# Second attention: key sums in two PSUM banks by turns, preparation and mixing on two shared ones, rows of q loaded place by place

## The chip, the cores and the metric

The program runs on one core of one Trainium2 chip. The metric is the device time of one execution in microseconds; lower is better. TensorE is called PE below, VectorE DVE, ScalarE ACT, GpSimd POOL; SP is the sync engine, whose queue issues most of the DMAs.

## The reference, cut to what matters

The program computes two layers over `x` of 4 batches x 512 tokens x 128: each layer is a layer norm, an attention `s`, a feed-forward net of 8 experts with two chosen, and `x = x + s * silu(ffn)`. The change touches the second layer's attention alone: 16 heads of width 8, and for each of 16 "wavelengths" a softmax of the same scores under another scale.

```python
def _L1_attn_ref(x, Wq, bq, Wk, bk, Wv, bv, Wo, bo, phase_modulators, interference_weights):
    Q, K, V = proj(Wq, bq), proj(Wk, bk), proj(Wv, bv)     # B, 16 heads, S, 8
    cos_pm = jnp.cos(phase_modulators)
    def wl_step(acc, wl):
        cpm, iw = wl
        m = cpm[None, :, None, None]
        scores = jnp.einsum('bhqd,bhkd->bhqk', Q * m, K * m) * SCALE
        scores = scores * jnp.cos(KERR * scores * scores)
        attn = jax.nn.softmax(scores, axis=-1)
        return (acc + jnp.einsum('bhqk,bhkd->bhqd', attn, V) * iw, None)
    ...
    return jnp.einsum('bse,ef->bsf', combined, Wo) + bo
```

## The kernel before

**What stands for the 16 softmaxes.** For small scores the exponential under every scale is a sum of six functions of the same score: three exponentials (of one, two and three times a fixed step) and the square, the score itself and one. So the kernel computes three arrays from each block of scores: `e0` by an exponential on ACT, `e1` as its square on ACT, `e2` as their product on DVE (line 1572), and sums each over the keys against V with a column of ones. The other three functions need no array per pair of query and key: the square of a score is a quadratic form in q, the score a linear one. `feat` holds the products of k's elements that this takes (5 shifts of 8 products, 8 linear ones and a one, in `ROWS1` = 49 columns), `forms` (line 1281) sums them over the keys against V into `lin`, `features1` (line 1326) makes the same products of q in `rows1`, and `bank1` (line 1348) multiplies the two. `sums1`, `quotients1` and `output1` then mix numerators and denominators over the wavelengths and apply `Wo`.

**Rounds.** `attn1` (line 1583) runs 64 rounds, 16 for a batch: round i stands for 4 heads (a group m of four) and 128 keys; 4 rounds make a group, 4 groups a batch. t is the round's place in its batch. In round i the program issues, each engine's part in this order: the scores of round i+1 (PE), the copy `bank0` of the last group's sums (DVE, where t is a multiple of 4), the evictions on ACT of what the last round's chunk left, the 24 instructions of `over_keys` (PE, the group `acc`), the chunk of this place, `e0` of i+1 (ACT), the rests on DVE and POOL of the last round's chunk, `e1` (ACT) and `e2` (DVE) of i+1. Where t is a multiple of 4, the chunk's PE part stands between the scores and `over_keys`.

**Chunks.** `prepare1` gives pieces for the next batch by place: token projections 0, 1 and 13, projections by head 2 and 3, `forms` 5, 7, 10 and 11. `mixing` gives `sums1` at 1 and 10, `quotients1` at 5, 6, 13 and 14, `bank1` at 8 and 15, `output1` at 9, partly for the batch before. Batch 0 has no mixing of a batch before, batch 3 no preparation.

**PSUM.** Of the eight banks, scores have four (tag `s`), the sums over keys one (`acc`), mixing two (`mix`), preparation one (`prep`). All engines keep the order in which the program records their instructions.

**Loads.** `project("q")` writes the transposed q to DRAM (`qe`, each head group twice in a row, so that shifted windows are contiguous). For each half batch `features1` loads `rows` (6 copies of 8 rows for each of two halves, 48 partitions) and `other` (5 shifted windows, 40 partitions), with 4 DMAs on SP, and the two operands are multiplied on POOL (line 1345). `operands1` loads q and k of a group (`q<-qd`, `k<-kd`), two groups ahead. `other` is one buffer for all halves. SP's queue takes its DMAs in order and holds all of them: parts of k and q (`kd`, `qd`), `qe`, `rows`, `other`, q, k and the output.

Of the kernel before, what the change touches and what calls it, by code (L numbers as in the profile page):

```python
# [12 lines left out]
F32 = mybir.dt.float32  # L13
# [52 lines left out]
LINEAR = SHIFTS * D1  # L66
ROWS1 = LINEAR + D1 + 1
# [30 lines left out]
class Kernel:  # L98
# [927 lines left out]
    def heads1(self, pool, keep):  # L1026


        nc = self.nc
        of = {}  # L1030
        for each in (32, WL):
            m = pool.tile([P, 4], F32, name=f"of{each}")
            nc.gpsimd.memset(m, 1.0)
            for at in range(0, P, each * 4):
                part = m[at : at + each * 4]
                nc.gpsimd.affine_select(
                    out=part, in_=part, pattern=[[-each, 4]], compare_op=ALU.is_ge, fill=0.0,
                    base=0, channel_multiplier=1,
                )
                nc.gpsimd.affine_select(  # L1040
                    out=part, in_=part, pattern=[[each, 4]], compare_op=ALU.is_ge, fill=0.0,
                    base=each - 1, channel_multiplier=-1,
                )
            of[each] = m


        self.count = keep.tile([P, 3], F32, name="count")
        ranges = (
            (0, SCALE1**2 * 2.0, ((D1, 4 * D1, SCALE1**2), (0, LINEAR, 0.0))),
            (1, SCALE1, ((LINEAR, LINEAR + D1, 0.0),)), (2, 1.0, ((LINEAR + D1, ROWS1, 0.0),)),  # L1050
        )
        for slot, value, limits in ranges:
            nc.gpsimd.memset(self.count[:, slot : slot + 1], value)
            for at in (0, HALF):
                part = self.count[at : at + HALF, slot : slot + 1]
                for first, end, fill in limits:
                    nc.gpsimd.affine_select(
                        out=part, in_=part, pattern=[[0, 1]], compare_op=ALU.is_ge, fill=fill,
                        base=-first, channel_multiplier=1,
                    )  # L1060
                    nc.gpsimd.affine_select(
                        out=part, in_=part, pattern=[[0, 1]], compare_op=ALU.is_ge, fill=fill,
                        base=end - 1, channel_multiplier=-1,
                    )
        return of
# [93 lines left out]
    def begin1(self):  # L1159

        nc, keep = self.nc, self.keep1
        self.bounds = keep.tile([P, 2 * B * H1 + 2], F32, name="bounds")

        self.feat = keep.tile([P, 4, H1, ROWS1], F32, name="feat")
        nc.gpsimd.memset(self.feat[:, :, :, ROWS1 - 1 : ROWS1], 1.0)
        self.sets1 = []
        for k in range(2):
            strip = keep.tile([P, 4, H1, STRIP], F32, name=f"strip{k}")
            nc.gpsimd.memset(strip, 0.0)
            nc.gpsimd.memset(strip[:, :, :, 26:27], 1.0)  # L1170

            lin = keep.tile([P, 2, 4, 32], F32, name=f"lin{k}")
            nc.gpsimd.memset(lin, 0.0)
            self.sets1.append((strip, lin))


        self.rows1 = [keep.tile([P, 4, S], F32, name=f"rows{mm}") for mm in range(2)]
        self.other1 = keep.tile([P, 4, S], F32, name="other")
        nc.gpsimd.memset(self.other1, 1.0)
        self.now1, self.banks1, self.inv1, self.prod1 = {}, {}, {}, {}  # L1180

    def prepare1(self, b, xnT, psum, tag):
# [9 lines left out]
        def tokens(w):  # L1192
# [9 lines left out]
            def rest(ps):  # L1202
# [13 lines left out]
                if w == "q":  # L1216
                    sq = pool.tile([P, 4 * H1, D1], F32, name=f"tsq{w}{b}", tag="tsq")
                    self.pool1(nc.gpsimd.tensor_mul(sq, t, t))
                    now["squares" + w] = sq
                    return  # L1220
                feat = self.feat.rearrange("p k h r -> p (k h) r")
                self.pool1(nc.gpsimd.tensor_copy(twice[:, :, D1 : 2 * D1], t))
                for d in range(SHIFTS):
                    self.pool1(nc.gpsimd.tensor_mul(
                        feat[:, :, d * D1 : (d + 1) * D1], t, twice[:, :, d : d + D1]
                    ))
                self.pool1(nc.gpsimd.tensor_copy(feat[:, :, LINEAR : LINEAR + D1], t))
                now["squares" + w] = feat[:, :, 0:D1]
# [13 lines left out]
        def project(w):  # L1242
# [10 lines left out]
            def rest(t):  # L1253
                if w == "q":

                    twice = now["twice"] = self.a1d.tile(
                        [4, 2 * D1, 4, S], F32, name=f"qe{b}", tag="qe"
                    )
                    for m in range(4):
                        for k in range(2):  # L1260
                            self.dma1(
                                twice[m, k * D1 : (k + 1) * D1].rearrange("d r s -> r d s"),
                                t[m * 32 : m * 32 + 32],
                            )
# [16 lines left out]
        def forms(mm, first):  # L1281
# [3 lines left out]
            def pe():  # L1285
                ps = psum.tile([P, 2, 9], F32, name=f"pl{b}_{mm}_{first}", tag=tag[0], bufs=tag[1])
                for r in heads:
                    for k in range(4):
                        for o in range(2):
                            h = (2 * mm + o) * 4 + r  # L1290
                            self.mm1(
                                ps[o * HALF : o * HALF + ROWS1, r - first],
                                lhsT=self.feat[:, k, h], rhs=strip[:, k, h, 18:27],
                                start=(k == 0), stop=(k == 3),
                            )
                return ps

            def rest(ps):
                for o in range(2):
                    rows = slice(o * HALF, o * HALF + ROWS1)  # L1300
                    self.vec1(nc.vector.tensor_tensor(
                        lin[rows, mm, first : first + 2, 0:27].rearrange(
                            "p r (x d) -> p r x d", x=3
                        ),
                        bc(ps[rows], 2, 3), bc(bc(self.count[rows], 1, 2), 3, 9), ALU.mult,
                    ))
# [4 lines left out]
            0: tokens("k"), 1: tokens("v"), 2: project("k"), 3: project("q"), 5: forms(0, 0),  # L1311
            7: forms(0, 2), 8: sizes("k"), 10: forms(1, 0), 11: forms(1, 2), 13: tokens("q"),
# [13 lines left out]
    def features1(self, b, mm):  # L1326

        nc, rows, other = self.nc, self.rows1[mm], self.other1
        for o in range(2):
            src, at = self.now1[b]["twice"][2 * mm + o], o * HALF  # L1330
            each = src[0:D1].rearrange("d r s -> d (r s)")
            self.dma1(
                rows[at : at + LINEAR + D1].rearrange("p r s -> p (r s)"), bc(each, 0, SHIFTS + 1)
            )

            (step, _), (one, n) = each.ap
            windows = bass.AP(
                tensor=each.tensor, offset=each.offset,
                ap=[[step, SHIFTS], [step, D1], [one, n]],
            )  # L1340
            self.dma1(other[at : at + LINEAR].rearrange("p r s -> p (r s)"), windows)

# [5 lines left out]
    def bank1(self, b, mm):  # L1348
# [17 lines left out]
        def evict(out):  # L1366
            for o, ps in enumerate(out):
                t = self.a1.tile([P, S], F32, name=f"bank1_{b}_{mm}_{o}", tag="bank1", bufs=3)
# [109 lines left out]
    def end1(self, b, g1):  # L1478
# [7 lines left out]
        den = psum.tile([P, 4, P], F32, name="dene", tag="prep")  # L1486
# [96 lines left out]
    def attn1(self, xnT, g1):  # L1583
# [4 lines left out]
        with tc.tile_pool(name="a1", bufs=2) as self.a1, tc.tile_pool(  # L1588
# [9 lines left out]
            def over_keys(i, f, ex):  # L1598
                b, m, k = i // 16, i // 4 % 4, i % 4
                if k == 0 and f == 0:  # L1600
                    self.acc = psum.tile([P, S], F32, name=f"acc{b}_{m}", tag="acc")
# [9 lines left out]
            def bank0(i):  # L1611

                t = pool.tile([P, S], F32, name=f"bank0_{i}", tag="bank0", bufs=3)
                self.vec1(nc.vector.tensor_copy(t, self.acc))  # L1614
# [22 lines left out]
            loads, makes = {1: [(0, 0)], 4: [(0, 1)]}, {2: [(0, 0, 0), (0, 0, 1)]}  # L1637
            for fb in range(B):
                if fb:
                    loads[fb * 16 - 7], loads[fb * 16 + 1] = [(fb, 0)], [(fb, 1)]  # L1640
                    makes[fb * 16 - 4], makes[fb * 16 - 3] = [(fb, 0, 0)], [(fb, 0, 1)]
                makes[fb * 16 + 6], makes[fb * 16 + 7] = [(fb, 1, 0)], [(fb, 1, 1)]
            waiting, late, prep, products = [], [], {}, {}
            large = self.large1(flag)
            for i in range(n):
# [8 lines left out]
                if t == 0:  # L1654
                    prep = self.prepare1(b + 1, xnT, psum, ("prep", 1)) if b + 1 < B else {}
                for fb, mm, half in makes.get(i, []):
                    products[fb, mm][half]()
                for fb, mm in loads.get(i, []):
                    if fb == 0:
                        for at in (ROWS1 - 1, HALF + ROWS1 - 1):  # L1660
                            self.dma1(self.rows1[mm][at : at + 1], self.other1[at : at + 1])
# [4 lines left out]
                if t % 4 == 0 and i:  # L1666
                    bank0(i)
                ready = evicted(waiting)
                chunks = [c for c in (mixing(b, t), prep.get(t)) if c]
                if t % 4 == 0:  # L1670
                    waiting = [(pe(), *more) for pe, *more in chunks]
                for f, e in enumerate((first, second, third)):
                    over_keys(i, f, e)
                if t % 4:
                    waiting = [(pe(), *more) for pe, *more in chunks]
# [6 lines left out]
                late = [f for f in [rest(x) for rest, x in ready] if f]  # L1682
                if nxt:
# [3 lines left out]
            bank0(n)  # L1687
# [429 lines left out]
```

## Time and profile before

| | us |
|---|---|
| median of 3 runs | 908.65 (904.13 to 909.3) |
| profiled execution, its span | 914.08, 912.0 |
| second attention, rounds 0 to 63 | about 533 to 890 of the span |
| PE busy (whole span) | 832.6, 91% |
| DVE, ACT, POOL busy | 597.1, 519.4, 387.5 |
| mean granted clock of PE | 0.963 |

Times are read against the span's start. A busy PE is not a PE at its peak, since matmuls are pipelined and their ends modelled; the two numbers that matter are when a round's first instruction starts and what an engine waited for before it. A group of instructions is named by what it writes and reads, as in `acc<-e,strip`: the sums over keys. Lines of 321, 324 and 333 are those of helpers that record every matmul, activation and DMA, so groups are told apart by their tiles. Durations by kind in this stage:

| instruction | line | mean us |
|---|---|---|
| `e0` and `e1`, ACT, 128x1024 | 324 | 1.02, 1.06 |
| `e2`, DVE, 128x1024 | 1572 | 1.485 (1.16 to 2.30) |
| `bank<-acc` copy, DVE | 1614 | 0.68 |
| reciprocal `inv`, DVE, 128x256 | 1393 | 1.75 |
| `rows<-rows,other`, POOL, 128x512 | 1345 | 1.70 (1.26 to 2.27) |
| `feat<-tokk`, POOL, 128x512 | 1224 | 1.61 (1.04 to 2.17 over the whole span) |
| issue of `rows<-qe`, `other<-qe`, `qe<-qT`, SP | 333 | 0.72, 0.73, 0.58 (medians) |

### The profile page before, as it was taken

How to read it: one execution, taken by the hardware profiler on the slowest of the kernel's cores; microseconds unless marked ns; L12 is line 12 of the kernel's file. 1: busy time of each engine (PE TensorE's matmuls, PEld its weight loads, DVE VectorE, ACT ScalarE, POOL GpSimd, SP SyncE). 2: the span in 40 equal slices, each digit the busy share in tenths (PEclk: the TensorE clock that was granted, in tenths of full speed). 3: DMA queues.
4: the chain of work that ended last, by engine and by line, in shares of the span. 5: the costliest groups of instructions: out<-in, count | busy, mean ns of one | idle time of the engine just before them, and what ended most of it. 6: DMA issues, size and time to landing. Idle time of an engine off the chain costs nothing. (4 is left out here: it accounts for less than half of the span.)

```text
span 912.0 us, 19106 instructions
## 1 busy us (share of the span) xinstructions
PE 832.6 (91%) x7724; PEld 511.1 (56%) x7724; DVE 597.1 (65%) x1170; ACT 519.4 (57%) x692; POOL 387.5 (42%) x469
## 2 busy tenths in 40 slices
PE   8998899999999999989999998559888989888886
PEld 4666788898897969866777742112232323222324
DVE  7764666666668868835534277538876877677574
ACT  3434465655656665534422388547766777677760
POOL 7840244545444434643060036327825492413212
PEclk9999899999999999999999999879998999899998
DMA  8502221212212121000031021362431243121000
GB/s 215 130 14 67 85 64 44 71 36 71 63 44 72 24 70 32 19 1 1 1 102 62 1 60 50 105 180 70 140 97 50 61 150 89 49 73 38 1 12 16
DMA packets 72719, 57.68 MB, mean 63 GB/s; under 512 B 40000, under 2 KB 64928, under 8 KB 71216
## 3 DMA queue, kind: packets, MB, share of 16 engines
q1 hardware_dynamic: 70432, 54.97, 21.2%
q0 software_dynamic: 1616, 1.16, 0.8%
q8 instruction: 63, 1.03, 0.5%
q10 hardware_dynamic: 576, 0.26, 0.1%
q14 instruction: 32, 0.26, 0.1%
HBM read 36.41 MB, written 19.92 MB: 62 GB/s over the span
## 5 line engine op out<-in xcount | busy, mean ns | idle before, releaser
L1572 DVE TENSOR_TENSOR e<-e,e 128x1024 f32<-128x1024 f32 x126 | 182.0, 1485 | 100.9 <-ACT e L324 98.9
L321 PE MATMUL acc<-e,strip 128*32 128x512 f32 x1520 | 197.8, 643 | 36.1 <-DVE bank L1614 35.6
L324 ACT ACTIVATE e<-s 128x1024 f32<-128x1024 f32 x126 | 122.2, 1024 | 99.0 <-PE s L321 99.0
L321 PEld LDWEIGHTS acc<-e,strip 128*32 128x32 f32 x1520 | 46.6, 115 | 156.3 <-issue 97.2
L324 ACT ACTIVATE e<-e 128x1024 f32<-128x1024 f32 x126 | 126.4, 1061 | 0.0
L324 ACT ACTIVATE h<-ph 128x1024 f32<-128x1024 f32 x32 | 32.8, 1024 | 84.5 <-PE ph L321 84.5
L1345 POOL TENSOR_TENSOR rows<-rows,other 128x512 f32<-128x512 f32 x32 | 53.4, 1699 | 45.7 <-DMA other<-qe 23.6
L324 ACT ACTIVATE pj<-pp 128x512 f32<-128x512 f32 x64 | 38.2, 596 | 52.4 <-PE pp L321 52.4
L321 PEld LDWEIGHTS eo<-w_out,h 128*128 128x128 f32 x512 | 60.9, 192 | 11.7 <-issue 10.4
L775 POOL TENSOR_TENSOR t<-t,gate 128x512 f32<-128x512 f32 x32 | 40.8, 1276 | 57.5 <-DVE t L708 40.7
L321 PE MATMUL eo<-w_out,h 128*128 128x128 f32 x512 | 63.2, 277 | 1.0 <-DVE g L974 0.8
L974 DVE SCALAR_TENSOR_TENSOR g<-eo,gw,g 128x128 f32<-128x128 f32 x112 | 31.5, 345 | 48.9 <-PE eo L321 48.9
L321 PE MATMUL dot<-vone,E 128*128 128x65 f32 x512 | 62.1, 275 | 0.0
L321 PEld LDWEIGHTS dot<-vone,E 128*128 128x128 f32 x512 | 60.6, 194 | 1.1 <-issue 0.8
L321 PE MATMUL ph<-xnT,w_in 128*128 128x512 f32 x128 | 60.3, 594 | 0.0
L321 PE MATMUL s<-q,k 64*128 64x512 bf16 x256 | 40.2, 388 | 20.0 <-DMA q<-qd 18.7
L727 POOL TENSOR_TENSOR t<-t,gate 128x512 f32<-128x512 f32 x32 | 41.0, 1280 | 35.4 <-DVE t L708 35.4
L750 DVE TENSOR_TENSOR mz<-mz,mu 64x512 f32<-64x512 f32 x56 | 38.3, 685 | 18.6 <-PE mu L321 18.0
L670 DVE SCALAR_TENSOR_TENSOR elu<-elu,up 128x512 f32<-128x512 f32 x60 | 43.3, 722 | 7.3 <-ACT up L324 6.4
L776 POOL TENSOR_TENSOR t<-t,t 128x512 f32<-128x512 f32 x32 | 45.4, 1419 | 2.5
L646 DVE TENSOR_TENSOR E<-sc,cap 128x1024 f32<-128x1024 f32 x32 | 39.1, 1220 | 10.2 <-PE sc L321 7.6
L324 ACT ACTIVATE attT<-pa 128x512 f32<-128x512 f32 x32 | 19.1, 597 | 45.8 <-PE pa L786 45.8
(275 smaller groups left out, 1537.1 us busy)
## 6 DMA issues: line engine op xcount, KB each, us to landing
vd<-vt SPq DMA_DIRECT2D x32, 256.0 KB
vone<-vd SPq DMA_DIRECT2D x64, 128.0 KB
rows<-qe SPq DMA_DIRECT2D x16, 384.0 KB
other<-qe SPq DMA_DIRECT2D x16, 320.0 KB
k<-kd SPq DMA_DIRECT2D x16, 256.0 KB
q<-qd SPq DMA_DIRECT2D x16, 256.0 KB
kd<-partk SPq DMA_DIRECT2D x12, 256.0 KB
qd<-partq SPq DMA_DIRECT2D x12, 256.0 KB
```

Of the source, the lines that this page charges most:

```text
L321: return self.pin(self.nc.tensor.matmul(*args, **kw))
L324: return self.pin(self.nc.scalar.activation(*args, **kw))
L646: self.vec1(nc.vector.tensor_tensor(e.rearrange("p x hp c -> p (x hp) c"), ps.rearrange("p x hp c -> p (x hp) c"), bc(self.cap.rearrange(" ...
L670: self.vec1(nc.vector.scalar_tensor_tensor(t, t, 1.0, up, ALU.min, ALU.add))
L727: nc.gpsimd.tensor_mul(t, t, self.gate)
L750: self.vec1(nc.vector.tensor_tensor(new[half, :, :, p, 0:DK], old[half, :, :, p, 0:DK], ps[half, :, :, p * 64 : p * 64 + 64].rearrange("d ...
L775: nc.gpsimd.tensor_mul(t, t, gate2)
L776: nc.gpsimd.tensor_add(t, t, seg[n]["t1"])
L974: self.vec1(v.scalar_tensor_tensor(acc[b][:, k, :], eo[:, k, :], w, acc[b][:, k, :], ALU.mult, ALU.add))
L1345: self.pool1(nc.gpsimd.tensor_mul(rows[:, r], rows[:, r], other[:, r]))
L1572: self.vec1(self.nc.vector.tensor_mul(t, src[0][pair], src[1][pair]))
```

## The change

The sums over keys get two banks and take them by turns, group by group. Preparation and mixing share the other two (tag `mix`), and some pieces of preparation move (5 to 4, 10 to 9, 13 to 12). Every chunk's PE part stands behind `over_keys`. The copy `bank0` is recorded behind the rests of its round and copies the bank that the last group left.

The order of the features changes: place j of 8 now holds shift j (0 to 4), the linear element (5) or a one (6 and 7), for each d, so `feat` has 64 columns, the rows of a half fill 64 partitions, and `lin` is made by one DVE operation over 128 partitions. `count` (the factor per row) is built by sums of the identity matrix instead of ranges. Rows of q are loaded place by place: 6 DMAs of 16 rows and 10 of 8 rows for a half batch, of 8 KB a row. q goes to DRAM three times (`qe` once, `qf` twice in a row), with 12 DMAs for 8. Loads and products of batch 0 move by a round or two. To make space, `bank1` has 2 buffers for 3, and the squares of q lie in the second half of their token tile.

```diff
-        den = psum.tile([P, 4, P], F32, name="dene", tag="prep")
+        den = psum.tile([P, 4, P], F32, name="dene", tag="acc", bufs=2)
...
-                    self.acc = psum.tile([P, S], F32, name=f"acc{b}_{m}", tag="acc")
+                    self.acc = psum.tile([P, S], F32, name=f"acc{b}_{m}", tag="acc", bufs=2)
...
-                    prep = self.prepare1(b + 1, xnT, psum, ("prep", 1)) if b + 1 < B else {}
+                    prep = self.prepare1(b + 1, xnT, psum, ("mix", 2)) if b + 1 < B else {}
...
-                if t % 4 == 0 and i:
-                    bank0(i)
-                ready = evicted(waiting)
-                chunks = [c for c in (mixing(b, t), prep.get(t)) if c]
-                if t % 4 == 0:
-                    waiting = [(pe(), *more) for pe, *more in chunks]
+                ready, before = evicted(waiting), getattr(self, "acc", None)
                 for f, e in enumerate((first, second, third)):
                     over_keys(i, f, e)
-                if t % 4:
-                    waiting = [(pe(), *more) for pe, *more in chunks]
+
+                waiting = [(pe(), *more) for pe, *more in filter(None, (prep.get(t), mixing(b, t)))]
...
                 late = [f for f in [rest(x) for rest, x in ready] if f]
+                if t % 4 == 0 and i:
+                    bank0(i, before)
```

```diff
-            0: tokens("k"), 1: tokens("v"), 2: project("k"), 3: project("q"), 5: forms(0, 0),
-            7: forms(0, 2), 8: sizes("k"), 10: forms(1, 0), 11: forms(1, 2), 13: tokens("q"),
+            0: tokens("k"), 1: tokens("v"), 2: project("k"), 3: project("q"), 4: forms(0, 0),
+            7: forms(0, 2), 8: sizes("k"), 9: forms(1, 0), 11: forms(1, 2), 12: tokens("q"),
...
-            loads, makes = {1: [(0, 0)], 4: [(0, 1)]}, {2: [(0, 0, 0), (0, 0, 1)]}
+            loads, makes = {}, {}
             for fb in range(B):
-                if fb:
-                    loads[fb * 16 - 7], loads[fb * 16 + 1] = [(fb, 0)], [(fb, 1)]
-                    makes[fb * 16 - 4], makes[fb * 16 - 3] = [(fb, 0, 0)], [(fb, 0, 1)]
-                makes[fb * 16 + 6], makes[fb * 16 + 7] = [(fb, 1, 0)], [(fb, 1, 1)]
+                at = fb * 16
+                for mm, load, make in (
+                    (0, at - 7 if fb else 1, at - 4 if fb else 3),
+                    (1, at + (1 if fb else 5), at + (6 if fb else 8)),
+                ):
```

```diff
-        self.feat = keep.tile([P, 4, H1, ROWS1], F32, name="feat")
-        nc.gpsimd.memset(self.feat[:, :, :, ROWS1 - 1 : ROWS1], 1.0)
+        self.feat = keep.tile([P, 4, H1, HALF], F32, name="feat")
+        nc.gpsimd.memset(self.feat, 1.0)
...
-                for d in range(SHIFTS):
-                    self.pool1(nc.gpsimd.tensor_mul(
-                        feat[:, :, d * D1 : (d + 1) * D1], t, twice[:, :, d : d + D1]
-                    ))
-                self.pool1(nc.gpsimd.tensor_copy(feat[:, :, LINEAR : LINEAR + D1], t))
-                now["squares" + w] = feat[:, :, 0:D1]
+                for j in range(SHIFTS):
+                    self.pool1(nc.gpsimd.tensor_mul(feat[..., j], t, twice[:, :, j : j + D1]))
+                self.pool1(nc.gpsimd.tensor_copy(feat[..., SHIFTS], t))
+                now["squares" + w] = feat[..., 0]
...
                     for m in range(4):
-                        for k in range(2):
-                            self.dma1(
-                                twice[m, k * D1 : (k + 1) * D1].rearrange("d r s -> r d s"),
-                                t[m * 32 : m * 32 + 32],
-                            )
+                        dst = [once[m], twice[m, 0:D1], twice[m, D1 : 2 * D1]]
+                        for d in dst:
+                            self.dma1(d.rearrange("d r s -> r d s"), t[m * 32 : m * 32 + 32])
...
-        for o in range(2):
-            src, at = self.now1[b]["twice"][2 * mm + o], o * HALF
...
+        once = now["once"].rearrange("m d r s -> (m d) (r s)")[mm * 16 : mm * 16 + 16]
+        for j in range(SHIFTS + 1):
+            self.dma1(places(rows)[:, j], once)
+        for j in range(SHIFTS):
+            for o in range(2):
+                src = now["twice"][2 * mm + o, j : j + D1].rearrange("d r s -> d (r s)")
+                self.dma1(places(other)[o * D1 : (o + 1) * D1, j], src)
```

## The prediction

> **What bounds the kernel now.** I read the page first: the chain that ended last and the costliest groups.
>
> ```profile
> PE 26%; DVE 6%; issue 3%; ACT 3%; DMA 2%; SPq 1%; ACTq 0%; DVEq 0%
> L321 PE MATMUL acc<-e,strip 128*32 128x512 f32 x1520 | 197.8, 643 | 36.1 <-DVE bank L1614 35.6
> ```
>
> PE carries the chain, and its largest group, the sums over keys of the second attention, is idle 36.1 us before its instructions, nearly all for one releaser: the copy `bank<-acc`. Then the table of waits from 526 to 892 us (who waited for whom: us in total, times, longest).
>
> ```profile
> PE acc L321 <- DVE bank L1614: 35.6, 15, 3.7
> PE s L321 <- DMA q<-qd: 18.7, 1, 18.7
> POOL rows L1345 <- DMA other<-qe: 23.6, 2, 15.8
> ```
>
> Two stalls of PE: 15 short ones, and one of 18.7 us for a load of q. Then the timeline of one round with the first stall and the two behind it (start, us, engine, line).
>
> ```profile
> 671.70 0.68 DVE L1614 COPY bank<-acc 128x512 f32<-128x512 f32 x1
> 672.43 4.48 PE L321 MATMUL acc<-e,strip 128*32 128x512 f32 x24 [2.52 <-DVE bank L1614]
> 676.85 0.61 PE L321 MATMUL s<-q,k 64*128 64x512 bf16 x4
> 677.38 2.78 PE L321 MATMUL acc<-e,strip 128*32 128x512 f32 x24
> 680.09 3.84 PE L321 MATMUL po<-wo_rep,pr 128*128 128x128 f32 x32
> 683.87 0.61 PE L321 MATMUL s<-q,k 64*128 64x512 bf16 x4
> 684.40 2.78 PE L321 MATMUL acc<-e,strip 128*32 128x512 f32 x24
> ```
>
> A round without a stall is PE work end to end: 0.53 us of scores, 2.71 of sums (677.38 to 680.09), and a chunk of preparation or mixing. A stall costs its 2.5 us twice: the sums behind it take 4.48 instead of 2.78 us, at a granted clock that the windows give as 0.65 (674 to 678 us). Last, the queue of DMAs and two windows around the long stall (in a window: length, busy PE, PEld, DVE, ACT, POOL, clock, DMA share, GB/s).
>
> ```profile
> 578.07 16.07 SPq L333 DMA_DIRECT2D qe<-qT  x8
> 597.54 0.70 SPq L333 DMA_DIRECT2D q<-qd  x1
> 588.00:590.00 2.00, 0.00 (x0) 0.00 (x0) 0.00 (x0) 0.00 (x0) 0.00 (x0) 0.51 0.33 113
> 596.00:598.00 2.00, 0.00 (x0) 0.00 (x0) 0.00 (x0) 0.00 (x0) 2.00 (x3) 0.50 1.03 345
> ```
>
> What matters is the last three columns. Eight issues of `qe` (5.1 us in later batches) take 16.1 while the four loads of `rows` and `other` in front of them use 0.33 of the DMA engines; loads with 128 outer rows use all. The loads of q and k that PE needs for round 12 stand behind them in SP's queue.
>
> **The sum: rounds.** From start of scores to start of scores, batches 0 to 3 of the second attention take 94.6 (531.99 to 626.58), 91.0, 89.0 and 83.2 us (to the end of the last sums, 889.8). The PE work in them: 16 rounds of 3.24 us = 51.8, and by starts in the timeline 3 token projections of 1.09, 2 head projections of 1.07, 4 `forms` of 0.85, 2 `bank1` of 1.09, 2 `sums1` of 1.8, 4 `quotients1` of 1.06, one `output1` of 3.78: 22.6. So 74.4 for batches 1 and 2, 66.7 for batch 0 (no mixing of a batch before: 7.7 less), 64 for batch 3 (no preparation, last scores and last `bank1` left out). Above that lie 78 us. The 15 rounds with a bank stall exceed their own PE work by 51.7 in all (0.7 to 6.3 each, the half-rate sums included), round 11 by 19.6 (25.55 against 5.98), the other 47 rounds together by about 7.
>
> **Two banks for the sums (removed wait).** `over_keys` of a new head group writes another bank, so it no longer waits for the copy; the copy moves behind the DVE rests of its round, and the bank is wanted again four rounds later (over 16 us, the copy takes 0.68). All chunks move behind the sums; PE order changes, not its work. So the 51.7 go; what is late next is ACT and DVE.
>
> ACT: one round is 3.82 us (`e` at 648.66 to 652.48), plus 0.6 per `bank1` tile, 0.69 per projection, 0.63 per gate: about 67 in batches 1 and 2, under PE's 74.4. In batch 3, 7 rounds have no chunk, and there 3.82 holds instead of 3.24: by the larger of both, round by round, 71, and 1 for waits: 72.
>
> DVE: busy 67.8 and 66.8 us in batches 1 and 2 as cut at 629.7, 720.1 and 809.1. It is in time on average, but not when POOL works: two products `e` take 2.36 us alone and 4.1 to 4.5 beside POOL's two-input operations, and today each bank stall lets DVE catch up. The second product is ready some 5.75 us after the scores (683.87 to 689.67) and wanted after 4.3 + 2.35 = 6.65, so 0.9 us of cover; where POOL works (about 10 of 16 rounds) it is gone. Unstalled rounds with POOL busy show an excess of 0.3 to 0.7 now (4.72 against 4.30 at 659.11). I take 10 rounds of 0.35: 3.5 a batch. Batches 1 and 2: 78 each, gains of 13 and 11; batch 3: 11.2.
>
> **Shared banks for preparation and mixing.** Each chunk now needs a bank that the chunk before left, freed by ACT or DVE a round later. Evictions take 0.4 to 0.7 us, `inv` 1.75 a half; the second half frees its bank 7.5 us after the scores, and PE comes for it 4.3 + 3.24 = 7.54 after them. No wait on average, up to 2 us at two places a batch beside POOL; it is inside the 3.5. The new places of the chunks (4, 9, 12 for 5, 10, 13) take turns with the two-bank ones, so no round waits for a round's own rest.
>
> **Loads place by place.** Per load of a half (8 in all): 16 issues for 4, the same 1,408 KB. Nothing in the trace issues 16 or 8 rows of 8 KB; nearest are `rows<-qe` at 0.72 us and `k<-kd` at 0.45. I take 0.72, the same kind: 11.5 us of SP for 2.9. `qe` becomes `qe` and `qf`: 12 issues for 8, 0.6 us each, 2.4 more. In batches 1 to 3 this is covered: the issues begin at place 1 or 9, the q and k behind them are wanted 5 rounds later (24 us), the products 3 to 5 rounds later.
>
> Batch 0 has no such cover. Its chain now, from rows: `feat` ends on POOL at 548.9; POOL then waits 7.8 us for the first half's loads today. Issued from 534.8, 17 loads end at 547, so POOL goes on at once; two products (3.5), three casts of k (7.8) to 560.2, two products, casts of q to 570.6. `kd`, `qe`, `qd` follow to 571.2; then 17 loads of the second half, 12 us, to 583; q and k of round 12 issue at 584 and, as today (597.54 to 602.25), land some 3 to 4.7 us later: 587. Without stalls PE asks at 531.99 + 46.3 = 578.3. So a stall of 8.7 us in place of 18.7, and 1.3 for the clock behind it. Batch 0: 66.7 + 3.5 + 10 = 80, a gain of 14.6. Bounds: at 0.45 an issue the stall is 4, at 0.82 it is 11.
>
> [...]
>
> **Small parts.** `feat` is written with a step of 8 floats, by POOL, 6 instructions a batch, 9.9 us beside DVE. No row shows such a step; `feat` today (runs of 8) takes 1.04 alone like `tsq`. Price: none, up to half as much again, 5 us, of POOL; it hides outside batch 0, where it would add 5 to the stall. I take none. [...] `forms` loads 64 columns for 49: 136 ns (row `den`) for 126, 32 times, 0.3 a chunk at most; 0 taken, since the matmuls pass at 26 ns each. `lin` is one DVE operation for two, 0.2 less. `count` is another handful of POOL operations near 40 us, as long as the 3.3 us removed. The larger memset of `feat` (twice `other`'s 1.84) falls in POOL's 38 us of idleness before 456 us. `bank1` with two buffers: read at places 10, 14 and 1, 6, written at 9 and 0, so free.
>
> **Sum.** 14.6 + 13 + 11 + 11.2 = 50 us off the profiled execution: 914.1 (912.0 of span, 2.1 around it) to 864. It stands 5.4 above the median of the three runs, 908.65; off that the forecast is **859 us**.
>
> **Rivals.** (1) *DVE is the bound.* If every round beside POOL loses 1 us and a shared bank adds to it, batches 1 and 2 take 84, batch 3 76, batch 0 87: 27 saved, 882. For it: 4.5 us products and no more rest; against: 67 of 78 us busy. 0.20. (2) *The loads do not go faster*: still 5 engines, SP held up, round 11 as long as today: 10 less, 869. Against: full share with 128 rows. 0.08. (3) *No stall is left*: issues at 0.45, POOL early, DVE in time: batches of 69, 75.5, 75.5, 70: 67 saved, 842. 0.12. (4) *SP becomes the bound, slower.* Were an issue 2.05 us, as one `rows<-other` at 572 took, a half costs 34 us: q and k come 12 late for round 8, 41 for round 12, 15 for round 16 (batch 0: 138), and SP has 32 x 2.05 + 22 = 88 us a batch in 1 and 2; 36 us slower, 945. It decides from about 1.6 us an issue, where gain and loss are even. Against: 0.70 to 0.82 for all 32 of the kind. 0.04. (5) *The change is right and the time stays*: each stall comes back one wait later (900 to 908). Against: unstalled rounds run at PE's own work now. 0.05. The forecast itself: 0.51, 850 to 872.
>
> **Numbers.** The range runs from rival 3 to rival 1: 841 to 884; outside it lie 4, 5 and the edges of both. About 1% (9 us) is what a measurement of this kernel can tell from no change. Faster by more: 0.51 + 0.20 + 0.08 + 0.12 less 0.01 for edges = 0.90; within 0.05; slower 0.05.
>
> **What would show it.** Right: no wait of `acc` for `bank`; rounds after a group's end of 3.2 to 4.4 us with sums of 2.78; batches of 76 to 80; one wait `s<-q` of 4 to 11 us in batch 0; 0.7 us an issue of `rows`, and 12 issues of `qe` and `qf` in about 7 us. Wrong: `acc` waiting for `e` of DVE in most rounds (rival 1); matmuls of chunks waiting for `pr`, `inv` or `tok`; SP busy through whole batches (rival 4).

## The result, and the profile after

The changed kernel takes 869.63 us (median of 4 runs, 867.35 to 869.99) beside 908.97 for the kernel before (4 runs, 904.13 to 914.12): a ratio of 0.956, 95% interval 0.951 to 0.962. That is 39 us less by the medians. Its profiled execution takes 869.38 us (span 867.3) against 914.08 (912.0), 45 us less.

The page first, with the two kinds of line that the prediction showed:

```profile
PE 25%; DVE 4%; POOL 3%; SPq 2%; issue 2%; ACT 1%; DMA 1%; ACTq 0%; DVEq 0%; POOLq 0%
...
L319 PE MATMUL acc<-e,strip 128*32 128x512 f32 x1520 | 195.1, 603 | 1.8 <-DVE e L1561 1.7
```

PE still carries the chain, now with POOL (3%) and more of SP's queue in it (SPq, 2% for 1%). The sums over keys are idle 1.8 us before their instructions instead of 36.1, and `bank<-acc` is no longer a releaser. The table of waits, 526 to 850 us (us in total, times, longest):

```profile
POOL rows L1334 <- DMA k<-kd: 13.4, 1, 13.4
...
PE s L319 <- DMA q<-qd: 6.0, 1, 6.0
...
PE acc L319 <- DVE e L1561: 1.7, 3, 1.2
...
PE ptq L319 <- DVE inv L1382: 1.2, 2, 0.6
```

The long wait of the scores for a load of q is down from 18.7 to 6.0 us. Short waits for DVE are what is left: of the sums for `e2` (one of 0.5 us before) and of the chunk `ptq` for `inv`. The timeline of the round that answers to the one shown before (the first of a group, and the one behind it):

```profile
655.91 0.68 DVE L1603 COPY bank<-acc 128x512 f32<-128x512 f32 x1
...
655.92 1.05 PE L319 MATMUL acc<-e,strip 128*32 128x512 f32 x4 [0.36 <-DVE e L1561]
...
657.92 0.60 PE L319 MATMUL s<-q,k 64*128 64x512 bf16 x4
...
658.46 2.94 PE L319 MATMUL acc<-e,strip 128*32 128x512 f32 x24
...
661.33 1.10 PE L319 MATMUL pl<-strip,feat 128*64 128x9 f32 x32
```

The copy runs while the sums of the new group are on PE already; PE waits 0.36 us, for the product `e2`. The sums that follow take 2.94 us; in the round shown before they took 4.48, behind the bank stall. And SP's queue in batch 0, second half of the rows of q, then the load that round 11 waits for:

```profile
576.15 3.73 SPq L331 DMA_DIRECT2D rows<-qe  x6
579.93 5.90 SPq L331 DMA_DIRECT2D other<-qf  x10
585.93 0.38 SPq L331 DMA_DIRECT2D k<-kd  x1
586.36 0.47 SPq L331 DMA_DIRECT2D q<-qd  x1
```

Sixteen issues take 9.7 us, about 0.6 each, and nothing holds SP up between them. Batches, cut as in the prediction (start of the second round's scores to the next batch's), in us from one profile each:

| us | batch 0 | 1 | 2 | 3 | first scores at |
|---|---|---|---|---|---|
| before | 94.6 | 91.0 | 89.0 | 83.2 | 526.3 |
| forecast | 80 | 78 | 78 | 72 | 526.3 |
| after | 80.9 | 80.5 | 79.1 | 71.4 | 527.8 |

Below, round k runs from the start of its own scores to the start of the next; so the chunk of place t lies in round t + 1 of its batch.

### The profile page after: what moved, and what is told of

The parts are those of the page before. It is cut to its first block, busy times and chain, and to the rows that moved or that the text cites. A ratio compares the mean times of both kernels' runs of the same rounds, so it can differ in the third digit from the quotient of the medians.

```text
span 867.3 us, 19179 instructions
## 1 busy us (share of the span) xinstructions
PE 833.5 (96%) x7724; PEld 514.7 (59%) x7724; DVE 603.2 (70%) x1154; ACT 519.2 (60%) x692; POOL 407.8 (47%) x463
## 3 DMA queue, kind: packets, MB, share of 16 engines
q0 software_dynamic: 1616, 1.16, 0.8%
## 5 line engine op out<-in xcount | busy, mean ns | idle before, releaser
L1561 DVE TENSOR_TENSOR e<-e,e 128x1024 f32<-128x1024 f32 x126 | 190.5, 1552 | 46.9 <-ACT e L322 46.9
L319 PE MATMUL acc<-e,strip 128*32 128x512 f32 x1520 | 195.1, 603 | 1.8 <-DVE e L1561 1.7
L1334 POOL TENSOR_TENSOR rows<-rows,other 128x512 f32<-128x512 f32 x32 | 59.7, 1894 | 25.8 <-DMA k<-kd 13.4
L972 DVE SCALAR_TENSOR_TENSOR g<-eo,gw,g 128x128 f32<-128x128 f32 x112 | 31.5, 344 | 49.5 <-PE eo L319 49.5
L748 DVE TENSOR_TENSOR mz<-mz,mu 64x512 f32<-64x512 f32 x56 | 38.4, 685 | 19.3 <-PE mu L319 18.7
L319 PE MATMUL s<-q,k 64*128 64x512 bf16 x256 | 39.3, 384 | 7.3 <-DMA q<-qd 6.0
```

Source lines behind the costliest of these rows:

```text
L319: return self.pin(self.nc.tensor.matmul(*args, **kw))
L748: self.vec1(nc.vector.tensor_tensor(new[half, :, :, p, 0:DK], old[half, :, :, p, 0:DK], ps[half, :, :, p * 64 : p * 64 + 64].rearrange("d ...
L972: self.vec1(v.scalar_tensor_tensor(acc[b][:, k, :], eo[:, k, :], w, acc[b][:, k, :], ALU.mult, ALU.add))
L1334: self.pool1(nc.gpsimd.tensor_mul(rows[:, r], rows[:, r], other[:, r]))
L1561: self.vec1(self.nc.vector.tensor_mul(t, src[0][pair], src[1][pair]))
```

## The experiments

**The kernel before, once more.**

> The kernel before, profiled a second time, to see what of the differences is only from execution to execution: where the second attention starts (first scores at 526.3 us in the first profile) and how long batches 0 to 3 take (94.6, 91.0, 89.0, 83.2). Theory 1 (the half-rate stretches behind the bank stalls fall differently in each execution): start within 1 us of 526.3 and batch times that differ from the first profile by up to 3 us each. Theory 2 (the profile is exact to a few tenths): the same batch times to 0.5 us, and the 1.5 us by which the second attention starts later in the changed kernel belongs to the change.

Measured: 912.35 us in one run, batches 93.2, 92.8, 88.9, 80.3, first scores at 526.25. The start repeats to 0.05 us, single batches to 3, as Theory 1 had it; so a batch that differs by less than 3 us between two kernels says little by itself.

**The banks alone.** The kernel before with these lines, the moved pieces of preparation, and the chunks and the copy behind the sums:

```diff
-                    self.acc = psum.tile([P, S], F32, name=f"acc{b}_{m}", tag="acc")
+                    self.acc = psum.tile([P, S], F32, name=f"acc{b}_{m}", tag="acc", bufs=2)
...
-                    prep = self.prepare1(b + 1, xnT, psum, ("prep", 1)) if b + 1 < B else {}
+                    prep = self.prepare1(b + 1, xnT, psum, ("mix", 2)) if b + 1 < B else {}
```

> The kernel before with the banks alone: two for the sums over keys, two shared by preparation and mixing, all chunks behind the sums, the copy behind the rests, pieces at 4, 9 and 12; features, loads and their rounds as before. Theory 1 (the bank stalls and the queue of loads are two separate costs): batches 1 to 3 as in the changed kernel, 80, 79 and 71 us, and batch 0 still held up in round 11, now longer, since PE comes earlier: 16 to 24 us for q, batch 0 about 95; about 884 us in all. Theory 2 (the loads also set the later batches): batches 1 and 2 stay above 85, about 895. Theory 3 (the banks are all of the gain and the loads move nothing): 870.

Measured: 878.94 us, ratio 0.965 (0.960 to 0.970); batches 94.9, 80.2, 79.6, 71.6. From its table of waits:

```profile
POOL rows L1345 <- DMA other<-qe: 23.4, 3, 15.0
...
PE s L321 <- DMA q<-qd: 19.6, 1, 19.6
```

Batches 1 to 3 are those of the changed kernel, so all of the gain there belongs to this part. In batch 0 it gives nothing: PE reaches round 12's scores earlier and waits there until the same load has come. That is Theory 1; the time lies 5 us below its 884, with 2.9 of that in an earlier start of the stage (523.4 for 526.3).

**The loads alone.** The changed kernel with the lines above undone: one bank, the old places, the old order.

> The changed kernel with the banks undone: one bank for the sums, one for preparation, the copy and the chunks where they were before, pieces at 5, 10 and 13; features in 64 columns and loads place by place stay. Theory 1: bank stalls as before in all batches, so batches 1 to 3 of about 91, 89 and 83; round 11 waits for q some 4 us and not 18.7; about 897 us in all. Theory 2 (place by place makes SP or POOL slower for all batches): batches 1 and 2 above 93, time 905 or more. Theory 3 (the loads move nothing): 909.

Measured: 897.53 us, ratio 0.984 (0.979 to 0.988); batches 80.9, 92.0, 88.9, 81.1.

```profile
PE acc L319 <- DVE bank L1603: 33.4, 14, 3.2
...
PE s L319 <- DMA q<-qd: 2.5, 1, 2.5
```

The mirror image: the bank stalls are back, and batch 0 is as short as with both parts, because what ends it is the load of q, not PE. Over the four batches the banks alone save 31.5 us, the loads alone 14.9, both together 45.9: the parts add up, since each acts in other batches. This holds within the noise only: against the second profile of the kernel before the same savings are 28.9, 12.3 and 43.3, and the medians, each against the kernel before in its own session, give 32.3, 13.7 and 39.3.

**Each load of rows cut in two.** As many bytes, twice the issues:

```diff
-            self.dma1(places(rows)[:, j], once)
+            for c in (slice(0, 1024), slice(1024, 2048)):
+                self.dma1(places(rows)[:, j, c], once[:, c])
```

and `other` in the same way.

> The changed kernel with every load of rows and other cut into two of half the row: 32 issues for a half batch, not 16, the same bytes. Theory 1 (an issue costs SP 0.6 us whatever its bytes, and batches 1 to 3 cover it): 9.7 us more on SP for each half; batch 0 longer by 10 to 20, since its chain goes through three halves, batches 1 to 3 unchanged within 1 us each: 880 to 890. Theory 2 (SP is close to its bound in the later batches too): batches 1 and 2 longer by 5 or more each. Theory 3 (the time goes with the bytes): no change, 869.

Measured: 881.18 us in one run; batches 96.7, 80.0, 81.1, 71.3. SP's queue for the second half of batch 0:

```profile
577.60 7.59 SPq L331 DMA_DIRECT2D rows<-qe  x12
585.24 12.11 SPq L331 DMA_DIRECT2D other<-qf  x20
...
597.88 0.47 SPq L331 DMA_DIRECT2D q<-qd  x1
```

With half the bytes an issue takes 0.63 and 0.61 us (7.59 over 12 and 12.11 over 20) for 0.62 and 0.59 in the changed kernel, so here SP pays for the issue and not for its bytes. Sixteen more issues a half cost 15.8 us in batch 0, as Theory 1 had it. Batch 1 differs by 0.4 and batch 2 by 2.0 us, which is inside what a batch repeats to: there the next loads have a cover of rounds.

**POOL's products left out.** The changed kernel without the products of `rows` from the second half of batch 1 on, and with one of five products of `feat` in batches 2 and 3.

> The changed kernel without part of POOL's work: from batch 1's second half on, the products of rows and other are left out, and for batches 2 and 3 four of the five products that make feat. Theory 1 (what batches 1 and 2 take above their PE work of some 75 us is DVE slowed by POOL): batches 1 and 2 fall from 80.5 and 79.1 to about 77, products e take 1.2 to 1.3 us where POOL has nothing to do, and PE's sums wait less for e. Theory 2 (it is the shared banks or the order on DVE alone): batches 1 and 2 stay at 79 to 80.5.

Measured: 864.28 us in one run; batches 81.3, 77.7, 76.9, 69.3. The products `e2` in the stretch 613 to 697 us (about batch 1), in the changed kernel:

```profile
L1561 DVE TENSOR_TENSOR e<-e,e 128x1024 f32<-128x1024 f32 x34 | 53.1, 1602 | 8.9 <-ACT e L322 8.9
```

and without POOL's products:

```profile
L1563 DVE TENSOR_TENSOR e<-e,e 128x1024 f32<-128x1024 f32 x36 | 51.2, 1463 | 11.2 <-ACT e L322 11.2
```

Mean 1602 against 1463 ns. Round 25 falls from 5.67 to 4.46 us and round 29 (the chunk `ptq`, behind `inv`) from 5.61 to 4.34. So at least 2.1 to 2.8 us of each of batches 1 to 3 (80.5, 79.1 and 71.4 in the changed kernel) are DVE slowed beside POOL. It is a lower bound, for POOL's other work stayed, and the changed kernel's own trace shows DVE late beside that too, as in round 17:

```profile
612.74 3.50 POOL L1412 TENSOR_TENSOR pr<-pr,pr 128x512 f32<-128x512 f32 x2 [1.76 <-DVE pr L1407]
613.29 4.04 DVE L1561 TENSOR_TENSOR e<-e,e 128x1024 f32<-128x1024 f32 x2
...
617.38 0.14 PEld L319 LDWEIGHTS acc<-e,strip 128*32 128x32 f32 x4 [0.66 <-DVE e L1561]
```

PEld is PE's loading of weights. The two `e2` take 4.04 us beside POOL's products `pr`; the last weights of the sums wait for the second, and the sums take 3.57 us for 2.78. In round 20 they take 3.23, in the same way beside the products and the copy of `feat`. Round 32 keeps its 5.25, where `bank1` needs both shared banks and the quotients of the round before have just left them; DVE's `pr`, which reads the second of them, had itself waited 1.39 us for POOL's `pr`.

**q and k of batch 0's last group earlier.** In round 4 of the program instead of round 6, and so ahead of the second half's rows in SP's queue:

```diff
-                    if b + m // 4 < B:
+                    if b + m // 4 < B and (b, m) != (0, 3):
                         self.operands1(b + m // 4, m % 4)
+                if i == 4:
+                    self.operands1(0, 3)
```

> The changed kernel with the q and k of batch 0's last group issued in round 4, ahead of qe, qf and the second half's rows, and not behind them in round 6. Theory 1 (the wait in round 11 is only their place in SP's queue): the 6.0 us wait for q and the slow sums behind it (2.5 us) go from round 11. The next in SP's queue are q and k of batch 1, behind the loads of rows that wait for POOL's products: they are issued near 600 us now and would be wanted near 600 too, so part of the gain, 3 to 6 us, comes back as a wait in round 15 or 16: 864 to 867 us. Theory 2 (nothing else is late): 861. Theory 3 (the wait is the transfer's own time or the writes to DRAM): as the changed kernel, 869.

Measured: 866.67 us, ratio 0.954 (0.950 to 0.957), its runs (864.40 to 868.40) overlapping those of the changed kernel; batches 79.7, 79.1, 80.2, 71.4. Round 11 falls from 11.24 to 5.13 us: its wait came from the place in SP's queue. But round 15 goes from 4.84 to 9.08 and round 16 from 4.58 to 7.14, as the first loads of batch 1, next in that queue, are late now. That is Theory 1.

**Those of batch 1's first group too**, in round 8 instead of 10.

> As the run before, and q and k of batch 1's first group are issued in round 8, ahead of the loads of rows of round 9. Theory 1 (place in SP's queue): no wait for q or k left in batch 0, batch 0 about 72 us for 80.9: 861 us. Theory 2: the products of the second half now come too late for bank1 of round 15, since its rows still land at about 589: a wait of PE for POOL of 2 to 6 us there, 864 to 866.

Measured: 864.05 us, ratio 0.951 (0.947 to 0.954); batches 71.9, 86.4, 80.2, 71.4. Batch 0 has no stall left, and 5.9 us of its gain of 9 come back in batch 1, all in round 18 (12.25 us for 6.21). The time is that of Theory 2 and the place is not: round 15, where it put the wait, takes 4.21. The timeline of round 18:

```profile
609.74 1.04 POOL L1216 TENSOR_TENSOR tokq<-tokq 128x512 f32<-128x512 f32 x1
...
610.81 0.69 DVE L1230 TENSOR_REDUCE sizeq<-tokq 128x64 f32<-128x512 f32 x1 [4.64 <-POOL tokq L1216]
...
612.31 3.14 DVE L1561 TENSOR_TENSOR e<-e,e 128x1024 f32<-128x1024 f32 x2
...
614.37 3.06 PE L319 MATMUL acc<-e,strip 128*32 128x512 f32 x8 [3.61 <-DVE e L1561]
```

Read upwards from PE: the sums wait for `e2`; `e2` stands on DVE behind `sizeq`; `sizeq` waited 4.64 us for the squares `tokq` of POOL; and POOL, which keeps its order too, had them behind products of `rows` that had waited 5.55 us (to 603.66) for loads.

**The products of batch 1's first half two rounds later**, so that the squares come first.

```diff
-                    (0, at - 7 if fb else 1, at - 4 if fb else 3),
+                    (0, at - 7 if fb else 1, at - (2 if fb == 1 else 4) if fb else 3),
```

> The kernel with both early loads (q and k of group 3 of batch 0 in round 4, of the first group of batch 1 in round 8), and the first half's POOL products of batch 1 recorded in rounds 14 and 15 instead of 12 and 13, so that the squares of q stand before them on POOL. Theory (what the early loads gave in batch 0 came back in batch 1 because POOL, in order, held the squares of q behind products that waited for their loads, and DVE, in order, held e2 behind the sums of those squares): the round of 12.25 us falls to 4.2 to 5.5, batch 0 stays at 72, batch 1 goes from 86.4 to 78 to 81, the others stay at 80 and 71; 856 to 860 us. Rival (DVE and POOL have too little slack at the turn from batch 0 to batch 1 whatever the order, so the wait moves to another round): batch 1 stays at 84 or more, 862 to 866 us.

Measured: 863.25 us, ratio 0.948 (0.945 to 0.951); batches 71.9, 83.3, 79.1, 71.4. DVE's wait for the squares is gone and round 18 takes 7.55 us, so that reading holds. The expected 4.2 to 5.5 could not have come: this round takes 6.2 in the kernel before and in the changed one. But rounds 17, 20 and 21 grew by 0.5 to 0.9 each, and batch 1 fell by 3.1 where 5 to 8 were expected: both expectations missed in part (the time is the rival's), and it cannot be told from that of the run before it. It is the lowest median of the study: its six runs (860.44 to 865.95) all lie below the four of the changed kernel, so loads of q and k further ahead in the queue do beat the changed kernel, by some 6 us.

**The same for batches 2 and 3** (`at - 2` for every batch but the first).

> As the run before, but the first half's POOL products of batches 2 and 3 too are recorded two rounds later (places 14 and 15 for 12 and 13). Theory (only batch 1's loads are late; from there on the products wait for nothing): batches 2 and 3 the same within 1 us, the time within 2 us of the run before, 856 to 860 us. Rival (products beside the squares of q cost DVE time in every batch, so spreading them helps): batches 1 and 2 of the four shorter by 1.5 us or more each, 853 to 856 us.

Measured: 864.90 us, ratio 0.951 (0.948 to 0.954); batches 71.9, 82.5, 81.6, 71.4. Nothing is gained. The time is within 2 us of the run before, as expected, but batch 2 is 2.5 us longer, which neither expectation had. Round 29 falls from 5.63 to 4.34, and round 32 rises from 5.25 to 6.71, for `bank1` now waits for DVE's quotients.

**Two banks, but the order of before** at places 0, 4, 8 and 12: the copy first in its round, the chunk in front of the sums.

```diff
+                if t % 4 == 0 and i:
+                    bank0(i, self.acc)
+                chunks = [c for c in (prep.get(t), mixing(b, t)) if c]
+                if t % 4 == 0:
+                    waiting = [(pe(), *more) for pe, *more in chunks]
```

> The changed kernel with its two banks for the sums, but the order of before at places 0, 4, 8 and 12: the copy of the last group's sums is recorded first in its round, and the chunk's PE part stands between the scores and the sums. Theory (the second bank alone takes the wait away; where the copy and the chunk stand doesn't matter): no wait of acc for bank, batches of 79 to 82, 79 to 82, 78 to 81, 70 to 73, 867 to 873 us. Rival (the order is part of the gain: with the chunk first, PE stands at the chunk's operands or its bank with ready sums behind it, and the copy delays what the rests of the round write on DVE): waits of 0.5 to 2 us of the chunks' matmuls for DVE or ACT at places 0, 4, 8 and 12, batches 1 to 3 longer by 1.5 to 4 us each, 875 to 882 us.

Measured: 889.89 us, ratio 0.977 (0.971 to 0.983); batches 85.1, 90.5, 87.6, 70.4. The theory failed: with both banks there, 20 us are lost again. The rival was right in kind and too small in size: in batch 1 PE waits 2.79 us for `lin` at place 8 and 4.50 for `inv` at place 12, where 0.5 to 2 were expected. Beside the loads alone (897.53 us), which have the same order, two banks for the sums give only 7.6 us; with the new order they give 27.9. Each of the next two runs puts back one half of the old order.

**Only the copy first.**

> The changed kernel with the copy of the last group's sums recorded first in its round, as before; the chunks stay behind the sums. Theory (of the 20 us that the run with the whole order of before lost, the chunk's place in front of the sums is the cause: it waits for what DVE still has to do, lin and inv, and the sums wait behind it): 867 to 873 us, batches within 1.5 us of the changed kernel's. Rival (the copy is the cause: 0.68 us of DVE in front of lin and inv of the round, at the places where DVE has no slack beside POOL): 876 to 886 us.

Measured: 867.68 us, ratio 0.954 (0.947 to 0.961); batches 81.0, 81.1, 80.8, 71.4. No difference that can be told; batch 2 is 1.7 us longer than in the changed kernel, a little more than the 1.5 expected.

**Only the chunk in front of the sums.**

> The changed kernel with the chunk's PE part between the scores and the sums at places 0, 4, 8 and 12, as before; the copy stays behind the rests of its round. Theory (the chunk's place is the cause): waits of b for lin at place 8 and of ptq for inv at place 12, 2 to 4.5 us each, the sums behind them longer too; batches 1 and 2 of 86 to 91, 884 to 892 us. Rival (the copy is the cause): 867 to 876 us.

Measured: 883.47 us, ratio 0.972 (0.964 to 0.980); batches 83.4, 85.4, 85.4, 70.4. The timeline at place 12 of batch 1:

```profile
676.89 0.61 PE L319 MATMUL s<-q,k 64*128 64x512 bf16 x4
...
679.60 1.74 DVE L1382 RECIPROCAL inv<-den 128x256 f32<-128x256 f32 x1
...
681.27 0.14 DVE L1295 TENSOR_TENSOR lin<-pl,count 128x54 f32<-128x54 f32 x1
...
681.40 2.08 PE L319 MATMUL ptq<-l1wqt,xnT 128*128 128x128 f32 x8 [3.90 <-DVE inv L1382]
...
683.41 3.81 PE L319 MATMUL acc<-e,strip 128*32 128x512 f32 x24
```

`ptq` needs a shared bank that the second half of `inv` frees at 681.3. In front of the sums, that wait of 3.9 us stops PE while 24 ready matmuls stand behind it, and `ptq` and the sums then run longer too (2.08 and 3.81 us for 1.16 and 2.78; in the trace the sums' weights load at 683.41, 684.26 and 685.12, some 0.85 us apart, and from 685.75 to 686.18 0.43 apart); this round takes 10.26 us. Behind the sums PE comes for the same bank some 3 us later and waits 0.6 (round 29: 5.61). So the chunk's place is worth 14 us alone, and 20 with the copy, which then stands in front of `lin` on DVE: the wait of `bank1` for `lin` at place 8 of batch 1 is 1.07 us without the copy in front and 2.79 with it. Batches and time lie some 0.5 below what the theory expected; the waits are where it put them, the one at place 8 smaller than its 2 us.

## Why the prediction was right, point by point

**The time** of 869.6 us lies in the range, in the upper part of the forecast's own case (850 to 872), 10.6 above 859. Half of that is the stage: the profiled execution came to 869.4 where the sum made it 864.1. The other half is the last step, taking 5.4 us off for the distance from profile to median: the profiled execution of before lay 5 us above the median of its runs, that of after at its own. In the nine other kernels with several runs it lay between 3.2 below and 3.3 above, so the 5.4 belonged to that execution and not to the kernel.

**Two banks for the sums.** Right that the wait goes, and 10.5, 9.9 and 11.8 us of batches 1 to 3 with it (forecast 13, 11, 11.2). But the prediction put this gain down to the second bank. "All chunks move behind the sums; PE order changes, not its work" was costed at nothing, and 14 to 20 us hang on it: with two banks and the old order 20 us come back, as waits of the chunks at places 8 and 12. The copy's own move was rightly taken as free.

**Shared banks and DVE beside POOL.** This is the mis-sized term. 3.5 us a batch were to hold both; batches 1 and 2 exceed the PE work of 74.4 by 6.1 and 4.7. In batch 1, against 4.33 us for a round with such a chunk: round 25 has 1.3 and round 29 also 1.3, both of which go with the products left out; round 32 has 0.9 for a shared bank, which doesn't; rounds 17, 20 and 24 have 0.8, 0.5 and 0.5, for `e2` late beside POOL by the trace; and `forms` has 0.8 in all, below. DVE late beside POOL is thus some 4 us in batch 1, 2.8 of them shown by leaving products out and the rest read from the trace; that alone fills the 3.5, and the shared bank and `forms`, which were to cost nothing more, lie on top. Batch 3 took 71.4 us for 72, partly by luck: the 71 put down to ACT and PE there is no floor, since without POOL's products the batch took 69.3.

**Loads place by place.** An issue took 0.6 us, between the ends of 0.45 and 0.82 and below the 0.72 taken; the 12 of `qe` and `qf` took 7.6 us, for about 7. POOL was slower than forecast by 2 us at `feat` (550.9 for 548.9) and 4 by the casts of q (574.9 for 570.6), SP faster by 1.5 in the second half's loads (10.5 for 12); so q was issued 2.4 us after the forecast's 584 and the scores began at 589.6. Some 1.5 us of this lateness is the later start of the stage (527.8 for 526.3). PE too came for the load later than forecast, at 583.6 for 578.3, since rounds 1 to 11 took 50.1 us without the wait and not 46.3. So the wait was 6.0 for 8.7, and the 3.5 us put down for late DVE in this batch fell in front of the load, where they shorten the wait and add little to the time: the sum counted them twice. Rounds 11 and 12 together exceed their work by 8.7 us, where 10 were put down; that batch 0 came to 80.9 for 80 is partly luck. That covers of rounds hide the issues in batches 1 to 3 is shown by the doubled issues (80.0, 81.1 and 71.3 us for 80.5, 79.1 and 71.4). The sum also lets SP go on at once behind these loads (12 us for 17, then q and k), which no run of the kernel before shows: none of its loads is of 16 or 8 rows of 8 KB. In the changed kernel's trace SP does go on: the sixteen issues from 576.15 take 9.7 us, and `k<-kd` follows at 585.93. The DMA share is 0.61 and 0.80 in two stretches in which loads of 16 rows were issued (536.5 to 539.5 and 576 to 579 us) and 0.42 over the loads of 8 rows (580 to 586 us), against 0.33 behind the old loads. The 5 engines of the second rival are that 0.33 of the 16 that the profile counts, an estimate.

**Small parts.** In this stage:

```profile
L1222 POOL TENSOR_TENSOR feat<-tokk 128x512 f32<-128x512 f32 x15 | 22.7, 1610 | 0.0
...
L1223 POOL COPY feat<-tokk 128x512 f32<-128x512 f32 x3 | 6.5, 2153 | 0.0
...
L1230 DVE TENSOR_REDUCE sizek<-feat 128x64 f32<-128x512 f32 x3 | 3.3, 1092 | 0.0
```

The products that write `feat` with a step of 8 floats cost what they did (1611 ns before). The copy that does so does not: 2153 ns for 646. The reduction that reads with this step takes 1092 for 677. So the step cost something in two instructions a batch out of seven, 1.9 us in all, where the prediction took none, with a bound of 5. `forms` took 0.2 us more a chunk (1.10 at 661.33 for 0.91 before), taken as nothing, with a bound of 0.3.

**The rivals.** DVE as the bound: PE waits for `e2` before sums 1.7 us in all, but the loads of weights inside the sums wait for `e2` 37 times, 20.5 us in all, where the usual gap between such loads is 0.33 (91.0 us over 273); that leaves some 8 us over the stage (an estimate from these numbers). So the sign of this rival is there, and it is small beside the 23 us by which its 882 lies above the forecast. Loads no faster: no, round 11 takes 11.24 us for 25.55. No stall left: only when q and k went ahead in the queue, and then part came back. SP as a bound: at the 0.6 us an issue that was measured, far from the 1.6 where it would decide; the doubled issues show the mechanism, 16 us in batch 0 alone. Its 36 us do not come out of the terms given: 138, 88, 88 and the 72 of batch 3 are 28 more than the kernel before takes. The change right and the time the same: not as it stands, but with the old order the stalls do come back at the next wait.

**What stays open.** The first scores start at 523.4 to 530.7 us in the kernels of this study, though the code ahead of them is the same or nearly so: the banks alone start 2.9 us earlier than the kernel before, which itself repeats to 0.05. Differences of some 3 us between two kernels' times can come from there; what makes them was not tried. That rounds 17 and 20 are late by DVE beside POOL is read from the trace; no run took that work of POOL's away.

## What to carry to other kernels

A buffer that two producers share is paid for by where the user stands: behind work that is ready, the wait for it was 0.6 us here; in front of that work, on an engine that keeps its order, it was 3.9 and stopped both. When one stall has a queue of loads behind it and another an engine, undo each alone: here the savings add up within the noise, as they act in different stretches. And when a load is moved forward in a queue, look at what stands behind it, and follow the waits through every in-order engine up to the one that sets the time.

## What the hardware showed beyond that

- SP spent 0.59 to 0.63 us on one issue in most sets of these loads, whether the load was 128, 64 or 32 KB; the longest set in the changed kernel took 0.81 each (4.84 for six). Here issues counted, and not bytes.
- The step of 8 floats in `feat` more than tripled a copy on POOL (646 to 2153 ns beside DVE; 642 to 1116 ns in the one copy that ran ahead of this stage), left POOL's products of two operands as they were (1611 and 1610 ns), and added six tenths to a reduction on DVE (677 to 1092 ns).
- A stall of PE was dearer than its wait in some rounds and not in others, and the wait's length did not settle it. In the kernel before, the sums behind bank waits of 2.52, 2.72 and 3.70 us took 4.48, 2.78 and 5.35 us, at granted clocks of 0.63, 1.00 and 0.50 in the stretches behind (672.4 to 677, 651.25 to 654 and 698 to 704 us). The sums ran longer behind a load too (4.82 us after 6.04) and behind a chunk in front (3.81 after 3.90).
